# Attention block over 16 images on one core: v's transpositions in eight parts, biases in the evictions, x loaded ahead of v

## The chip, the cores and the metric

The kernel runs on one core of one Trainium2 chip. The metric is the device time of one execution in microseconds; lower is better. A core has five engines that work at the same time, each through its own queue and in order: TensorE (PE) multiplies matrices, VectorE (DVE) and ScalarE (ACT) work elementwise, GpSimd (POOL) and SyncE (SP) here mostly issue transfers.

## The reference

Group normalisation, attention over the 1,024 pixels of each image, projection, residual. Cut to what matters:

```python
# x: (16, 512, 32, 32) float32; 4 heads of 128 channels, 8 groups
xg = x.reshape(b, 8, -1)
h = (xg - mean(xg)) / sqrt(var(xg) + 1e-5)      # then * gamma + beta, per channel
qkv = qkv_w @ h + qkv_b                         # (1536, 512) weights, 1x1 convolution
q, k, v = split(qkv)                            # each 4 heads x 128 x 1024
p = softmax(q.T @ k * scale)                    # 1024 x 1024 per head
o = v @ p.T
out = x + proj_w @ o + proj_b
```

## The kernel before

**Score steps.** The main loop (around L2230) runs over images b, heads h and key blocks j: step s = 32 b + 8 h + j. A step has two halves, one for each half of the 1,024 queries. A half issues a score matmul (L1600), its exponential on ScalarE (L1606), the weighted sum with v of the step before (`po`, L1697), and then "halfway" units: matmuls of other products, which share TensorE with attention. VectorE adds the exponentials up to the softmax's divisor (`tot`, L1621). At the end of a head the divisor is turned (L1630, L1632 and on), spread by transfers, and divides `o` (L1710).

**The other products.** q, k, v of the next image and the projection of the last one are made by Strassen's scheme, seven products in place of eight, on two levels. Images 1 to 3 take q, k, v with two levels of it (`two_levels`). From image 4 on (`OLD = 4`) `thirds` makes q, k, v in two pairs of heads, eight groups per pair (`G` = 0 to 15), with x in three column ranges of 342, 342 and 340. A group is seven units in the order p1, p2, p6, p5, p7, p4, p3. ScalarE empties some of the accumulators (L1156, L1160, L1163; for the projection L634, L650, L802): with a copy, or with an activation that adds a bias where `BIASED` says so. VectorE adds others at L1221 (in `thirds`) or L804 (in `two_levels`). The last of a group is c22 = y + u3: p3 accumulates on the bank that c22 reads, so TensorE cannot start p3 before that addition has ended.

The groups' results `r` are added up by outer additions (`combine`; L1284, L1293). They form q and k directly; for v they form `vt` by L1306, one instruction for each row of channels, which also adds v's bias. `turn_v` turns `vt` by 32 x 32 blocks on VectorE (L1017), writes it to DRAM (`vd`, L1025) and reads it back into `v` (L1030), both on POOL's queue. All four transpositions of a pair are put into the list `pending` at the pair's group 6; the list is worked off unit by unit, and what is left of the second pair runs with the last unit of group 15.

**When.** The groups for image b + 1 begin at head 2 of image b and go on until head 1, key block 0, of image b + 1 itself; the first pair's group 7 falls in head 3, key block 4. The projection of image b - 1 (`proj_groups`, four groups) runs in head 1 of image b. `prepare` loads the residual from x in DRAM, 256 KB each; `finish` (L1569 to L1576) adds result, bias and residual (L1572), the second part (L1575), and stores (L1576). In the same head the next x is loaded on POOL's queue (`load_x`, L289), its sums are taken by ScalarE (L325 to L331), group statistics by VectorE (L353 to L365, one power on POOL at L359), and then x is normalised in place by ScalarE (L108) after the shift `sh` (L101). The order on each engine is that of the program text, but for the places where the text gives a priority or puts an instruction behind another.

**Pools that the change touches.** `xpool`: x as two tiles of two channel chunks; `ypool`: four single tiles of 128 x 512, shared by `vu`, residuals and early weights; `vt` in `opool`.

Of the kernel before, what the change touches and what calls it, by code (L numbers as in the profile page):

```python
# [208 lines left out]
BIASED = {0: (0, -1), 5: (2, 1), 14: (0, 1), 12: (2, 1)}  # L209
# [20 lines left out]
def fast_path(ctx, tc, x, sources, out, consts, flag, dims):  # L230
# [16 lines left out]
    xpool = ctx.enter_context(tc.tile_pool(name="x", bufs=KC))  # L247
# [8 lines left out]
    ypool = ctx.enter_context(tc.tile_pool(name="y", bufs=4))  # L256
# [22 lines left out]

    def load_x(b, chunks=range(NCC)):  # L280
        for c in chunks:
            if c % KC == 0:
                xw[b, c // KC] = xpool.tile([P, KC, N], F32, tag="x", name=f"x_{b}_{c // KC}")
            xs[b, c] = xw[b, c // KC][:, c % KC, :]
# [96 lines left out]

    def halves(tiles, prefix):

        b = {
            f"b{r + 1}{h + 1}": [tiles[2 * r + k][:, ts(h, HALF)] for k in range(KC)]
            for r in range(2) for h in range(2)
        }
        b["t1"] = b["b12"]
        for n in ("t2", "t3", "t4"):
            if prefix == "x":  # L390
                t = tpool.tile([P, KC, HALF], F32, tag="f", bufs=3, name=f"x{n}")
                b[n] = [t[:, k] for k in range(KC)]
                continue
            b[n] = [
                tpool.tile([P, HALF], F32, tag=f"{prefix}{n}{k}", name=f"{prefix}{n}{k}")
                if n == "t4" else home["A"][:, 2 * (int(n[1]) - 2) + k]
                for k in range(KC)
            ]
        return b
# [153 lines left out]
    def stage_v():  # L553
# [4 lines left out]
        for n in ("a21", "a22", "s4"):  # L558
            t = ypool.tile([P, HALF], F32, tag="y", name=f"wv_{n}")
            wv[n] = t.rearrange("p (k m) -> p k m", m=HC)  # L560
# [9 lines left out]
    def keep_kept(site, part, eng):  # L570
# [8 lines left out]
        if part == 0 and site == "proj":  # L579
            beside["s4"] = ypool.tile([P, HALF], F32, tag="y", name=f"k{site}_s4").rearrange(  # L580
                "p (f d) -> p f d", d=P
            )
# [105 lines left out]
    def two_levels(name, site, b, blocks, finish, sums="make", homes="BBBB", prepare=None):  # L688
# [59 lines left out]
        def group_units(g):  # L748
# [31 lines left out]
            def out_(which, a, c=None):  # L780
# [16 lines left out]
                with (  # L797
# [3 lines left out]
                    if c is None:  # L801
                        nc.scalar.copy(dst, view(a))  # L802
                    else:
                        latest["outer"] = nc.vector.tensor_add(dst, view(a), view(c))  # L804

            p1, p2, p6, p5, p7, p4, p3 = strassen(
                f"{name}_{g}", mm, out_, n * Q, seeded=not (b == 0 and site in range(PAIRS))
# [43 lines left out]
        def ready(g):  # L851
            for which in results.get(g, ()) if prepare else ():
                for r in range(2):
                    prepare(which, r)
# [11 lines left out]
        def done(which, i, j):  # L866
            pending.extend(
# [128 lines left out]
    def v_groups(b):  # L996
# [3 lines left out]
        def finish(which, h, a, c):  # L1000
            pair, half = int(which[1]) - 1, int(which[2]) - 1
            t = ypool.tile([P, HALF], F32, tag="y", name=f"vt_{b}_{pair}_{h}_{half}")
            i = 2 * pair + h
            nc.vector.scalar_tensor_tensor(t, a, vb_sb[:, i : i + 1], c, ALU.add, ALU.add)
            turn_v(b, pair, half, h, t, rows)
# [3 lines left out]
    def turn_v(b, pair, half, h, t, rows):  # L1009
        which = half  # L1010
        if (b, pair) not in vs:
            vs[b, pair] = vpool.tile(
                [P, NH2, 2, P, NB // NH2], F32, tag="v", name=f"v_{b}_{pair}"
            )
        n = P // BLK
        u = ypool.tile([P, HALF], F32, tag="y", name=f"vu_{b}_{pair}_{h}_{half}")
# [4 lines left out]
        if h == 0:  # L1021
            rows[which] = dpool.tile(
                [2 * P, HALF], F32, tag="v", name=f"vd_{b}_{pair}_{half}"
            )
        nc.gpsimd.dma_start(rows[which][ts(h, P), :], u)  # L1025
        if h == 0:
            return

        for q in range(n):
# [4 lines left out]
                rows[which].rearrange("(k m) (q e) -> q m k e", m=BLK, q=n)[q],  # L1034
            )

    def wide_x(b, r, n):
        return xw[b, r][:, :, ds(S3[n], W3)]

    def thirds(b):  # L1040

        first = b == old
        R, forms, made, sums, wts, rows, vts = {}, {}, {}, {}, {}, {}, {}
        pending, waiting = [], []
        late["heads"] = False
        count = len(THIRDS)
# [7 lines left out]
        def block(G, i, r, ch):  # L1054

            f = THIRDS[G % count][i]
            if f in RAW_B:
                row, n = RAW_B[f]
                return xw[b, row][:, r, ds(S3[n] + ch * H3, H3)]
            return forms[G][:, r, i, ts(ch, H3)]  # L1060

        def all_blocks(G, r, ch):
            return forms[G][:, r, : size(G), ts(ch, H3)]
# [25 lines left out]
        def make_sum(G, m):  # L1089
# [10 lines left out]
            def of(what, i=None):  # L1100
                if what[0] == "t":
                    return sums[G, what] if i is None else sums[G, what][:, i, :]
                r, ch = int(what[1]) - 1, int(what[2]) - 1
                return all_blocks(G, r, ch) if i is None else block(G, i, r, ch)

            with ExitStack() as order:
# [40 lines left out]
        def evict(dst, src, row, G):  # L1147
# [10 lines left out]
            for i, f in enumerate(group):  # L1158
                if f not in BIASED:
                    nc.scalar.copy(dst[:, i, :], src[:, i, :])  # L1160
                    continue
                m, sign = BIASED[f]
                nc.scalar.activation(  # L1163
                    dst[:, i, :], src[:, i, :], AF.Identity, bias=column(m, p, row, sign)
                )

        def column(m, p, row, sign=1):
            k = (HEADS if m else 0) + KC * p + row
            return negq[:, k : k + 1] if sign < 0 else qkb_sb[:, k : k + 1]
# [15 lines left out]
        def group_units(G):  # L1185
# [70 lines left out]
            def unit(k):  # L1256
                def one():
# [9 lines left out]
                    if G == 2 * count - 1 and k == len(us) - 1:  # L1267
                        run(f for _, f in pending)
# [3 lines left out]
            return [unit(k) for k in range(len(us))]  # L1272

        def combine(G):
# [13 lines left out]
            def final(m, n, add, i, j, frees=()):  # L1288
# [13 lines left out]
                def v(row):  # L1302
                    k = KC * p + row
                    if (p, row) not in vts:
                        vts[p, row] = opool.tile([P, N], F32, tag="o", name=f"vt_{b}_{p}_{row}")
                    nc.vector.scalar_tensor_tensor(  # L1306
                        vts[p, row][:, ds(S3[n], W3)], at(i, row), vb_sb[:, k : k + 1],
                        at(j, row), ALU.add, ALU.add if add else ALU.subtract,
                    )
                    if row:  # L1310
                        free(*frees)

                if m == 1:
                    pending.extend((G, lambda row=row: v(row)) for row in range(2))
                else:
                    pending.append((G, q_or_k))

            def alone(m, n, i, scale):

                def one():  # L1320
                    head_tiles(b, p)
                    for row in range(2):
                        dst = qw[b, p][m // 2][:, row, ds(S3[n], W3)]
                        nc.scalar.activation(
                            dst, at(i, row), AF.Identity, bias=column(m, p, row), scale=scale
# [10 lines left out]
            def turn(half, h):  # L1336
                def one():
                    turn_v(b, p, half, h, vts[p, h][:, ts(half, HALF)], rows_of_v)
                pending.append((G, one))
# [5 lines left out]
            elif g == 2:  # L1345
                op(False, 4, 2, 4, (2,))
                final(1, 0, True, 8, 3, (8,))
                op(True, 7, 7, 4)
                alone(2, 2, 7, -1.0)
# [3 lines left out]
            elif g == 4:  # L1353
                final(1, 2, False, 6, 4, (4,))
                op(False, 11, 11, 6, (6,))
            elif g == 5:
# [4 lines left out]
            elif g == 6:  # L1361
                final(1, 1, False, 10, 9, (10,))
                op(True, 9, 9, 13)
                rows_of_v = {}
# [13 lines left out]
    negq = one.tile([P, HEADS], F32, name="negq")  # L1378
# [118 lines left out]
    def lay_builder():  # L1497
# [7 lines left out]
        at(HEADS, 4, lambda: nc.scalar.mul(negq, qkb_sb[:, :HEADS], -1.0))  # L1505
# [37 lines left out]
    def proj_groups(b):  # L1543
# [3 lines left out]
        def place(which, r):  # L1547
            return 2 * (int(which[1]) - 1) + r, int(which[2]) - 1

        def prepare(which, r):  # L1550
            o, half = place(which, r)

            own = which == "c12"
            t = ys[which, r] = (tpool if own else ypool).tile(
                [P, HALF], F32, tag=f"ot4{r}" if own else "y", name=f"y_{b}_{o}_{half}"
            )

            eng = nc.sync if own else nc.gpsimd
            dma = eng.dma_start(t, x[b, ts(o, P), ts(half, HALF)])
# [9 lines left out]
        def finish(which, r, a, c):  # L1569
            o, half = place(which, r)  # L1570
            t = ys.pop((which, r))
            nc.vector.scalar_tensor_tensor(  # L1572
                t, a, projb_sb[:, o : o + 1], t, ALU.add, ALU.add
            )
            nc.vector.tensor_add(t, t, c)  # L1575
            latest["sent"] = nc.gpsimd.dma_start(out[b, ts(o, P), ts(half, HALF)], t)  # L1576
# [177 lines left out]
    def last_loads(what):  # L1754


        if what == "x":
            late["y"] = []
            for c in range(NCC):
                if c % KC == 0:  # L1760
                    two = xpool.tile([P, KC, N], F32, tag="x", name=f"y_{c // KC}")
                t = two[:, c % KC, :]
# [152 lines left out]
    def plan_head(b, h):  # L1915
# [23 lines left out]
        elif h == 1:  # L1939
            if b > 0:  # L1940
                spread(plan, [None] * 28, 0, NB)
                halfway.extend([flow.pop() if flow else []] + paced(proj_groups(b - 1), 3))
            if b + 1 == B:
                plan[0].append(lambda: last_loads("x"))
            else:
# [3 lines left out]
                spread(plan, [lambda c=c: stats_chunk(b + 1, c) for c in chunks], *at)  # L1949
# [280 lines left out]
    for s in range(steps + 1):  # L2230
# [15 lines left out]
        for half in range(NH2):  # L2246
# [23 lines left out]
            run(extras.pop((s, half), ()))  # L2270
        if s < steps and h == 1 and j == 6 and 0 < b < B - 1:
# [150 lines left out]
```

## Time and profile before

| | |
|---|---|
| median of 3 runs | 3164.6 us (3163.41 to 3168.26) |
| profiled execution: time, span | 3165.8 us, 3164.3 us |
| TensorE busy | 3122.8 us, 99% |
| VectorE busy | 2723.2 us, 86% |
| ScalarE busy | 1683.8 us, 53% |
| GpSimd busy | 520.8 us, 16% |
| data moved | 632.69 MB, 200 GB/s |
| granted TensorE clock | 9 tenths or more in all 40 slices |

Times are microseconds from the start of the span. In the timeline a row reads: start, time to the last end, engine, line, operation, output <- inputs, number of instructions run together, and in brackets the idle time before with what ended it. A matmul of this program is two records. Records of one engine overlap by a few hundredths to some tenths of a microsecond, so a duration is longer than the distance to the next start. In the waits a row reads: who waits, for whom, total, times, longest.

### The profile page before, as it was taken

The page shows a single profiled execution, that of the slowest core. Times are in us where ns is not written, and L with a number is a line of the kernel's source. Part 1 is how long each engine was busy: PE and PEld are TensorE (multiplying, and loading weights), DVE is VectorE, ACT ScalarE, POOL GpSimd, SP SyncE. Part 2 cuts the span into 40 slices and gives each one's busy share as a digit, 9 for nine tenths or more (in the row PEclk, how much of TensorE's full clock was granted, in tenths as well). Part 3 has the DMA queues.
Part 4 walks back from the last instruction along what each step waited for, and adds up shares of the span by engine and source line. Part 5 has one row for each costly group of instructions (what it writes and reads, how often), then busy time and mean ns, then how long its engine had stood idle before and what let it go on. Part 6 is the DMA issues. An engine that isn't in the chain of part 4 may idle for free. (4 is left out here: it accounts for less than half of the span.)

```text
span 3164.3 us, 38443 instructions
## 1 busy us (share of the span) xinstructions
PE 3122.8 (99%) x11934; PEld 2260.2 (71%) x11934; DVE 2723.2 (86%) x4792; ACT 1683.8 (53%) x3529; POOL 520.8 (16%) x935
## 2 busy tenths in 40 slices
PE   9999999999999999999999999999999999999999
PEld 7566676767677777677776777777777776777775
DVE  9988888789898897988979889798897988979797
ACT  3545446455464555655556555465554656546543
POOL 0121121111021110211112111121111112111110
PEclk9999999999999999999999999999999999999999
DMA  5565765656766666676666666666666665666651
GB/s 176 176 222 169 246 201 174 201 176 195 240 224 217 201 196 197 221 216 197 197 195 224 210 199 201 199 220 209 195 207 200 213 216 189 215 199 210 213 195 46
DMA packets 245713, 632.69 MB, mean 200 GB/s; under 512 B 35184, under 2 KB 80368, under 8 KB 245504
## 3 DMA queue, kind: packets, MB, share of 16 engines
q1 hardware_dynamic: 165152, 363.59, 37.7%
q0 software_dynamic: 67680, 232.26, 20.8%
q10 hardware_dynamic: 12672, 34.35, 3.3%
q8 instruction: 96, 1.57, 0.2%
q14 instruction: 113, 0.93, 0.1%
HBM read 458.36 MB, written 171.69 MB: 199 GB/s over the span
## 5 line engine op out<-in xcount | busy, mean ns | idle before, releaser
L1697 PE MATMUL po<-p,v 128*128 128x512 f32 x2048 | 1045.4, 592 | 0.0
L1600 PE MATMUL s<-qk,qk 128*128 128x512 f32 x2048 | 1045.1, 592 | 0.0
L1606 ACT ACTIVATE p<-s 128x512 f32<-128x512 f32 x1024 | 611.8, 597 | 533.3 <-PE s L1600 529.0
L1697 PEld LDWEIGHTS po<-p,v 128*128 128x128 f32 x2048 | 615.9, 301 | 374.8 <-issue 258.6
L1621 DVE TENSOR_TENSOR tot<-tot,p 128x1024 f32<-128x1024 f32 (+1 forms) x408 | 472.5, 1159 | 130.4 <-ACT p L1606 128.6
L1600 PEld LDWEIGHTS s<-qk,qk 128*128 128x128 f32 x2048 | 361.4, 189 | 54.6 <-issue 26.8
L1221 DVE TENSOR_TENSOR r<-t_y,t_u 128x342 f32<-128x342 f32 (+1 forms) x384 | 186.0, 484 | 122.9 <-PE t_y L1197 88.2
L1025 POOL DMA_DIRECT2D vd<-vu x120 | 65.7, 549 | 1122.6 <-DVE vu L1017 1113.2
L1284 DVE TENSOR_TENSOR r<-r,r 128x684 f32<-128x684 f32 x264 | 226.3, 865 | 2.0 <-DVE r L1221 0.5
L1197 PE MATMUL t_x<-home_A,w 128*128 128x171 f32 x1008 | 187.9, 308 | 1.8 <-DVE w L1471 1.8
L1197 PE MATMUL t_x<-home_B,w 128*128 128x171 f32 x1008 | 187.7, 308 | 0.0
L1197 PEld LDWEIGHTS t_x<-home_A,w 128*128 128x128 f32 x1008 | 161.5, 189 | 32.6 <-issue 19.9
L1197 PEld LDWEIGHTS t_x<-home_B,w 128*128 128x128 f32 x1008 | 161.6, 189 | 30.4 <-issue 19.9
L775 PE MATMUL pp_x<-home_B,w_proj 128*128 128x256 f32 x630 | 168.3, 384 | 12.0 <-ACT pp_u L634 12.0
L1156 ACT COPY t_u<-t_x 128x342 f32<-128x342 f32 (+1 forms) x240 | 100.1, 417 | 145.1 <-PE t_x L1197 134.1
L775 PEld LDWEIGHTS pp_x<-home_B,w_proj 128*128 128x128 f32 x630 | 117.2, 190 | 56.1 <-ACT pp_u L634 29.9
L1030 POOL DMA_DIRECT2D v<-vd x240 | 139.7, 589 | 82.2 <-DMA vd<-vu 39.5
L1576 POOL DMA_DIRECT2D out_y<-y x120 | 65.7, 548 | 461.5 <-DVE y L1575 453.9
L1197 PEld LDWEIGHTS t_z<-f,w 128*128 128x128 f32 x528 | 89.5, 190 | 51.9 <-issue 34.4
L1017 DVE STREAM_TRANSPOSE vu<-vt 128x512 f32<-128x512 f32 x120 | 123.3, 1104 | 1.2 <-DMA vd<-vu 1.1
L1197 PE MATMUL t_y<-f,w 128*128 128x171 f32 x528 | 102.8, 312 | 17.1 <-DVE r L1221 17.0
L108 ACT ACTIVATE x<-x,sh,sc 128x512 f32<-128x512 f32 x120 | 94.4, 815 | 35.4 <-DVE sh L101 33.7
(394 smaller groups left out, 5111.6 us busy)
## 6 DMA issues: line engine op xcount, KB each, us to landing
w<-kept SPq DMA_DIRECT2D x178, 512.0 KB, 3.9
w<-kept SPq DMA_DIRECT2D x178, 384.0 KB, 3.9
kept_t<-home_A POOLq DMA_DIRECT2D x96, 342.0 KB, 4.1
home_B<-kept_t SPq DMA_DIRECT2D x96, 342.0 KB, 3.0
rinv<-row ACTq DMA_DIRECT2D x63, 512.0 KB, 5.0
x<-in_x POOLq DMA_DIRECT2D x60, 512.0 KB, 6.2
vd<-vu POOLq DMA_DIRECT2D x120, 256.0 KB, 4.2
v<-vd POOLq DMA_DIRECT2D x240, 128.0 KB, 5.2
```

What stands on the lines that cost most here:

```text
L108: return self.nc.scalar.activation(xn, x, AF.Identity, bias=sh[:, i], scale=sc[:, i])
L775: latest["product"] = nc.tensor.matmul(acc[:, ts(i, Q)], have["w"][t][:, i, slot, :], inner(i, bn), start=(first and i == 0), stop=True, s ...
L1017: nc.vector.transpose(u.rearrange("p (q i j) -> p j q i", q=n, i=BLK), t.rearrange("p (j q i) -> p j q i", q=n, i=BLK),)
L1030: nc.gpsimd.dma_start(vs[b, pair][ts(q, BLK), half].rearrange("m h (k i) j -> m (h k) (i j)", k=n), rows[which].rearrange("(k m) (q e) -> ...
L1156: nc.scalar.copy(dst, src)
L1197: latest["product"] = nc.tensor.matmul(acc[:, ts(i, H3)], wts[G, t][:, i, slot, :], moving, start=(start and i == 0), stop=True, skip_grou ...
L1221: nc.vector.tensor_add(dst, view(a), view(c))
L1284: (nc.vector.tensor_add if add else nc.vector.tensor_sub)(at(o), a, c)
L1600: latest["score"] = nc.tensor.matmul(sc, ks[b, h][:, ts(j, P)], qs[b, h][:, ts(half, HALF)], start=True, stop=True)
L1606: exps[s] = nc.scalar.activation(ps[s][:, ts(half, HALF)], sc, AF.Exp, scale=SCALE)
L1621: added[b, h, j] = nc.vector.tensor_add(tot[b, h][:, i], tot[b, h][:, i], ps[s][:, i])
L1697: summed = nc.tensor.matmul(po[half], v_block(b, h, j), ps[s][:, i], start=(j == 0), stop=(j == NB - 1),)
```

## The change

- *Biases.* v's bias and the projection's bias are added when ScalarE empties the accumulators: `BIASED` gets more entries, with sums and differences of the q, k and v biases made once (`sum_biases`); `BIASED_PROJ` and `empty` do it for the projection. The accumulators of the groups concerned are emptied in two instructions, one per factor. The final addition for v becomes one plain addition of 128 x 684 for both rows; the projection's `finish` becomes two plain additions of 128 x 1024.
- *Transpositions of v.* Eight parts of 256 columns per pair: for both rows, part 0 after group 2, part 3 after group 4, parts 1 and 2 after group 6. `vt` and `vu` hold both rows; `vd` is written in transfers of 512 KB.
- *Residual and output* move in four transfers of 512 KB per image in place of eight of 256 KB, in two tiles of the pool and one own tile (`ot4`).
- *x* lies in one tile, `every_x`; differences of blocks that lie in x itself are one instruction of 128 x 342 instead of two of 128 x 171.
- *Order.* Loads of the next x are issued ahead of the second pair's reads of v; what is pending after group 15 runs two per half; the projection begins half a step earlier; the statistics' sums are put behind an exponential.

```diff
-BIASED = {0: (0, -1), 5: (2, 1), 14: (0, 1), 12: (2, 1)}
+BIASED = {0: "-q-v", 2: "v", 3: "v", 5: "k+v", 12: "k-v", 14: "q+v"}
+BIASED_PROJ = {2: 0, 3: 0, 7: 1}
...
-    ypool = ctx.enter_context(tc.tile_pool(name="y", bufs=4))
+    ypool = ctx.enter_context(tc.tile_pool(name="y", bufs=2))
...
+            def empty(dst, src, row):
...
+                if not prepare or not any(f in BIASED_PROJ for f in group):
+                    nc.scalar.copy(dst, src)
+                    return
+                for i, f in enumerate(group):
+                    if f not in BIASED_PROJ:
+                        nc.scalar.copy(dst[:, i, :], src[:, i, :])
+                        continue
+                    o = KC * BIASED_PROJ[f] + row
+                    nc.scalar.activation(
+                        dst[:, i, :], src[:, i, :], AF.Identity,
+                        bias=projb_sb[:, o : o + 1],
+                    )
...
-                if g in FORMS_B:
-                    nc.vector.tensor_sub(to, of(a), of(c))
-                else:
-                    for i in range(n):
-                        nc.vector.tensor_sub(to[:, i, :], of(a, i), of(c, i))
+                nc.vector.tensor_sub(to, of(a), of(c))
...
                     if G == 2 * count - 1 and k == len(us) - 1:
-                        run(f for _, f in pending)
+                        late["tail"] = [f for _, f in pending]
...
+        def turn_part(p, h, part):
+            half, q = divmod(part, 2)
...
+            nc.vector.transpose(
+                u[:, h].rearrange("p (q i j) -> p j q i", q=n, i=BLK)[:, ds(2 * q, 2)],
+                made["vt"][:, h, ts(part, Q)].rearrange("p (j q i) -> p j q i", q=n, i=BLK),
+            )
...
+            nc.gpsimd.dma_start(rows.rearrange("(h p) e -> p h e", h=KC), u)
...
+            if p == 0:
+                back()
+            else:
+                late["reads"].append(back)
...
-                    nc.vector.scalar_tensor_tensor(
-                        vts[p, row][:, ds(S3[n], W3)], at(i, row), vb_sb[:, k : k + 1],
-                        at(j, row), ALU.add, ALU.add if add else ALU.subtract,
+                    (nc.vector.tensor_add if add else nc.vector.tensor_sub)(
+                        made["vt"][:, :, ds(S3[n], W3)], at(i), at(j)
                     )
...
+                turn(0)
...
+                turn(3)
...
-                for half in range(NH2):
-                    for h in range(2):
-                        turn(half, h)
                 alone(0, 1, 9, 1.0)
+                turn(1, 2)
...
-            dma = eng.dma_start(t, x[b, ts(o, P), ts(half, HALF)])
+            dma = eng.dma_start(t, place(which)(x))
...
-            nc.vector.scalar_tensor_tensor(
-                t, a, projb_sb[:, o : o + 1], t, ALU.add, ALU.add
-            )
+            nc.vector.tensor_add(t, a, t)
             nc.vector.tensor_add(t, t, c)
...
-                halfway.extend([flow.pop() if flow else []] + paced(proj_groups(b - 1), 3))
+                halfway.extend(paced(proj_groups(b - 1), 3))
+                if flow:
+                    halfway[0] = flow.pop() + halfway[0]
...
-                spread(plan, [lambda c=c: stats_chunk(b + 1, c) for c in chunks], *at)
+                spread(plan, [
+                    lambda c=c: behind_exp(lambda: stats_chunk(b + 1, c)) for c in chunks
+                ], *at)
...
+            for _ in range(2):
+                if late.get("tail"):
+                    late["tail"].pop(0)()
+            if h == 1 and j > 0 and late.get("reads"):
+                run(late.pop("reads"))
```

More of the change, by code (lines that the diff above doesn't have):

```diff
@@ L394, in halves @@
             b[n] = [
[L395 to L398, printed above, removed]
+                home["A"][:, 2 * (int(n[1]) - 2) + k] for k in range(KC)
+            ] if n != "t4" else list(map(own_t4().__getitem__, ((slice(None), k) for k in range(KC))))
         return b
@@ L852, in ready @@
             for which in results.get(g, ()) if prepare else ():
-                for r in range(2):
-                    prepare(which, r)
+                prepare(which)
         pending = []
@@ L1021, in turn_v, with read_v @@
         if h == 0:
-            rows[which] = dpool.tile(
+            rows[half] = dpool.tile(
                 [2 * P, HALF], F32, tag="v", name=f"vd_{b}_{pair}_{half}"
             )
-        nc.gpsimd.dma_start(rows[which][ts(h, P), :], u)
-        if h == 0:
-            return
+        nc.gpsimd.dma_start(rows[half][ts(h, P), :], u)
+        if h == 1:
+            read_v(b, pair, half, rows[half])
+    def read_v(b, pair, half, rows):
+        n = P // BLK
+        if (b, pair) not in vs:
+            vs[b, pair] = vpool.tile(
+                [P, NH2, 2, P, NB // NH2], F32, tag="v", name=f"v_{b}_{pair}"
+            )
         for q in range(n):
@@ L1334, in alone, with turn @@
                 pending.append((G, now))
[L1336 to L1339, printed above, removed]
+            def turn(*parts_):
+                for h in range(2):
+                    for part in parts_:
+                        pending.append((G, lambda h=h, part=part: turn_part(p, h, part)))
             if g == 1:
@@ L1377, in fast_path, with sum_biases @@
     home_c = tpool.tile([P, 4 * H3], F32, tag="homeC", name="home_C")
-    negq = one.tile([P, HEADS], F32, name="negq")
+    biases = {"v": vb_sb}
+    for what in ("q+v", "-q-v", "k+v", "k-v"):
+        biases[what] = one.tile([P, HEADS], F32, name=f"bias_{len(biases)}")
+    def sum_biases():
+        q, k = qkb_sb[:, :HEADS], qkb_sb[:, HEADS:]
+        nc.vector.tensor_add(biases["q+v"], q, vb_sb)
+        nc.vector.tensor_scalar_mul(biases["-q-v"], biases["q+v"], -1.0)
+        nc.vector.tensor_add(biases["k+v"], k, vb_sb)
+        nc.vector.tensor_sub(biases["k-v"], k, vb_sb)
     for p_ in range(PAIRS):
```

147 lines of the change are left out of this document (86 added, 61 removed).

## The prediction

> **What bounds the kernel now.** I read the page's busy shares first, then the waits of TensorE, then the timeline of each place where TensorE waits.
>
> ```profile
> PE 3122.8 (99%) x11934; PEld 2260.2 (71%) x11934; DVE 2723.2 (86%) x4792; ACT 1683.8 (53%) x3529; POOL 520.8 (16%) x935
> ```
>
> ```profile
> PE t_y L1197 <- DVE r L1221: 17.9, 26, 1.9
> PE pp_x L775 <- ACT pp_u L634: 12.0, 24, 0.7
> ```
>
> TensorE bounds the whole span, and the change leaves its matmuls as they are. So the change can earn only what TensorE waits for, or spend by making new waits. Two waits carry nearly all: the last unit of a group of q/k/v (a `t_y` matmul), which needs the addition c22 that VectorE makes at L1221, and the last units of the projection, which need a copy by ScalarE. Both are queues being late, not engines being full: VectorE works in order, and what is put ahead of c22 delays it. The waits repeat in each image at three places, which I call A, B and C.
>
> **Place A** (head 3, key block 4, the last unit of the first pair's group 7). VectorE's timeline, then TensorE's:
>
> ```profile
> 1975.44 2.99 DVE L1017 STREAM_TRANSPOSE vu<-vt 128x512 f32<-128x512 f32 x3
> 1978.29 1.20 DVE L1621 TENSOR_TENSOR tot<-tot,p 128x1024 f32<-128x1024 f32 x1
> 1979.42 1.08 DVE L1017 STREAM_TRANSPOSE vu<-vt 128x512 f32<-128x512 f32 x1
> ...
> 1981.13 0.48 DVE L1221 TENSOR_TENSOR r<-t_y,t_u 128x342 f32<-128x342 f32 x1
> ```
>
> ```profile
> 1980.23 0.46 PE L1197 MATMUL t_x<-home_A,w 128*128 128x171 f32 x2
> 1980.52 0.74 PE L1197 MATMUL t_x<-x,w 128*128 128x171 f32 x4
> 1981.67 0.85 PE L1197 MATMUL t_y<-f,w 128*128 128x171 f32 x4 [0.40 <-DVE r L1221]
> 1982.35 1.02 PE L1600 MATMUL s<-qk,qk 128*128 128x512 f32 x2
> ```
>
> Instructions overlap, so I count from start to start. Two records take 0.29 us (1980.23 to 1980.52), four 0.58; `t_y` was due at 1981.10 and came at 1981.67. It then takes 0.68 instead of 0.58. The wait costs 0.57 + 0.10 = 0.67 us. It occurs once for each of the 12 images whose q/k/v go this way, the first time shorter: about 7.7 us. What is ahead of c22 is four transpositions, 2.85 / 3 = 0.95 each.
>
> **Place B** (head 1, key block 0, the last unit of the second pair's group 15):
>
> ```profile
> 2045.64 1.06 DVE L1306 SCALAR_TENSOR_TENSOR vt<-r,vb_sb,r 128x342 f32<-128x342 f32 x2
> 2046.73 0.87 DVE L1284 TENSOR_TENSOR r<-r,r 128x684 f32<-128x684 f32 x1
> 2047.52 3.93 DVE L1017 STREAM_TRANSPOSE vu<-vt 128x512 f32<-128x512 f32 x4
> 2051.27 1.23 DVE L1621 TENSOR_TENSOR tot<-tot,p 128x1024 f32<-128x1024 f32 x1
> ...
> 2053.41 0.50 DVE L1221 TENSOR_TENSOR r<-t_y,t_u 128x342 f32<-128x342 f32 x1
> ```
>
> ```profile
> 2052.78 0.31 PE L1197 MATMUL t_x<-home_B,w 128*128 128x171 f32 x1
> 2053.97 0.85 PE L1197 MATMUL t_y<-f,w 128*128 128x171 f32 x4 [0.89 <-DVE r L1221]
> 2054.66 1.02 PE L1600 MATMUL s<-qk,qk 128*128 128x512 f32 x2
> 2055.51 1.02 PE L1697 MATMUL po<-p,v 128*128 128x512 f32 x2
> ```
>
> Due at 2052.93 (one record, 0.145), come at 2053.97: 1.04 + 0.10 = 1.15 us, 12 times, 13.8 us.
>
> **Place C** (head 1, key blocks 5 to 7, the projection's last two groups). ScalarE, TensorE, VectorE:
>
> ```profile
> 1899.01 0.81 ACT L108 ACTIVATE x<-x,sh,sc 128x512 f32<-128x512 f32 x1 [2.64 <-DVE sh L101]
> 1899.73 0.35 ACT L634 COPY pp_u<-pp_x 128x256 f32<-128x256 f32 x1
> 1899.98 0.81 ACT L108 ACTIVATE x<-x,sh,sc 128x512 f32<-128x512 f32 x1
> ```
>
> ```profile
> 1896.43 0.59 PE L775 MATMUL pp_z<-o,w_proj 128*128 128x256 f32 x2
> 1896.86 0.59 PE L775 MATMUL pp_x<-home_B,w_proj 128*128 128x256 f32 x2
> ...
> 1899.01 0.59 PE L775 MATMUL pp_y<-home_B,w_proj 128*128 128x256 f32 x2
> 1900.13 0.70 PE L775 MATMUL pp_x<-home_B,w_proj 128*128 128x256 f32 x2 [0.53 <-ACT pp_u L634]
> ...
> 1902.99 0.70 PE L775 MATMUL pp_x<-home_B,w_proj 128*128 128x256 f32 x2 [0.45 <-ACT pp_u L634]
> ```
>
> ```profile
> 1891.68 0.19 DVE L354 STREAM_TRANSPOSE groups<-table 128x64 f32<-128x64 f32 x1
> 1891.79 0.38 DVE L740 TENSOR_TENSOR home_B<-o 128x256 f32<-128x256 f32 x1
> 1892.18 0.78 DVE L356 COPY groups<-groups 32x64 f32<-32x64 f32 x4
> ...
> 1893.61 1.01 DVE L357 BATCH_NORM_AGGREGATE groups<-groups 128x2 f32<-128x192 f32 x1
> ...
> 1901.35 1.29 DVE L1575 TENSOR_TENSOR y<-y,pp_r 128x512 f32<-128x512 f32 x2
> ```
>
> The copies stand behind normalisations of the next x (L108). A projection matmul takes 0.43 (1896.43 to 1896.86); the one due at 1899.44 came at 1900.13. With its slower start that is 0.79 us; the second wait costs about 0.71 and two small ones the rest, in all 1.88 us per image, in 11 images (the first of them 1.23): 20 us. A, B and C are 41.5 us.
>
> **The change, part by part.** Further rows:
>
> ```profile
> L1163 ACT ACTIVATE t_u<-t_x,qkb_sb 128x171 f32<-128x171 f32 x144 | 52.8, 403 | 52.1 <-PE t_x L1197 52.1
> L1324 ACT ACTIVATE qk<-r,qkb_sb 128x342 f32<-128x342 f32 x96 | 54.6, 582 | 10.4 <-DVE r L1284 10.4
> L325 ACT ACTIVATE junk<-x 128x1024 f32<-128x1024 f32 x60 | 63.3, 1055 | 3.6 <-DVE part L1632 2.6 <-DMA x<-in_x 0.7
> ```
>
> ```profile
> x<-in_x POOLq DMA_DIRECT2D x60, 512.0 KB, 6.2
> ...
> out_y<-y POOLq DMA_DIRECT2D x120, 256.0 KB, 3.0
> ...
> y<-in_x POOLq DMA_DIRECT2D x90, 256.0 KB, 4.9
> ```
>
> *Transpositions of v.* Four of 128x512 per pair become eight of 128x256; two run after group 2, two after group 4 and four after group 6. Only those four still stand ahead of c22 at A and at B. No row shows a 128x256 transposition of this layout. It lies between 0.11 us (128x64, 1891.68 to 1891.79) and 0.94 (128x512: 2047.52 to 2051.27 is 3.75 for four). A line through the two gives 0.47; I take 0.49, as the small one is the nearer row in form but not in stride. Four cost 1.96 instead of 3.75: 1.8 us less ahead of c22.
>
> [...]
>
> *Bias of v.* Two L1306 of 128x342 (2045.64 to 2046.73, 1.06 busy, spaced 0.49) become one addition of 128x684, 0.79 (2046.73 to 2047.52): 0.2 us less. The bias goes into ScalarE's evictions, which must be split for it. A biased 171-wide one lasts 0.40, a 342-wide one 0.58, a 256-wide one so about 0.49 (an estimate), 0.39 start to start, beside 0.25 for its plain half (1899.73 to the 1899.98 at which L108 goes on). ScalarE is at 53% and waits for TensorE before most evictions, so the 3 to 4 us that this adds per image are hidden except where a copy is awaited within its own time; I find no such place outside C and set 0, with 0.2 us per image as the upper bound.
>
> *A and B after.* c22 can start 1.8 + 0.2 = 2.0 us earlier as far as VectorE's queue goes. The stalls were 0.57 and 1.04. Both go, with the slow first matmul behind each: 7.7 + 13.8 = 21.5 us. Next late is the copy that c22 itself reads, which at other groups leaves over half a microsecond. The two transpositions after group 4 come before c22 of group 5; there 0.98 new less what vt saves leaves an estimated 0.2 us in hand. After group 12 the queue has idle time before its next sum, so nothing follows:
>
> ```profile
> 1837.25 1.22 DVE L1621 TENSOR_TENSOR tot<-tot,p 128x1024 f32<-128x1024 f32 x1 [2.46 <-ACT p L1606]
> ```
>
>
> *Projection: bias in the eviction, 128x1024 residual additions, half a step earlier; statistics behind the exponential.* Eight plus eight additions of 128x512 become four plus four of 128x1024, bias and residual in one chain. In the new order the normalisations of x no longer stand before the last copies, so C's waits on ScalarE go. But VectorE's order is new: from the exponential of key block 4's second half on there stand ahead of c22 of the projection's last group the sum tot, the division of o, the halves' addition and four residual additions (7 x 1.13, the spacing 1978.29 to 1979.42), a memset and small transposition 0.14, c12 0.60 (1.29 - 0.69 of the L1575 pair), four copies 0.8, the aggregate 0.93, small ones 0.37; with c22's own 0.42, 11.2 us. TensorE, from the end of that score, has 9 passes of 0.85 (2054.66 to 2055.51) and 10 matmuls of 0.43 until it needs c22: 12.0 us. The exponential ends between 0.6 us after its score, if ScalarE is free, and 1.7, behind a copy's two parts (0.64) and a statistics pass (1.05, L325). The order puts both ahead, so I take 1.7: c22 is 0.9 us late, with the slow start 1.0 to 1.1. Bounds 0 and 1.6. C goes from 1.88 to 1.1 in 11 images: 20 - 12 = 8 us saved.
>
> *Loads.* x ahead of the second pair's v: ScalarE waited 0.7 us in all for x, so earlier x earns nothing. The v reads come some 2 us later on POOL's queue, but v of the second pair is used from head 2 on, over 30 us later. Fewer, larger stores and loads: nothing, hidden by the same distance, except in the second rival. *Last outer additions two per half, merged differences, one x tile:* VectorE's work off the critical path; 0.
>
> **Sum.** 7.7 + 13.8 + 8 = 29.5 us. The profiled execution took 3165.8 us (span 3164.3); the median of the runs is 1.2 below. 3165.8 - 29.5 = 3136.3: I say 3136.
>
> **Rivals.**
> *1. A half-size transposition costs what a full one does*, 0.94. Then only vt's 0.2 is saved: A waits 0.42 + 0.10, B 0.85 + 0.10, group 5 gets a new wait of about 0.75, C stays at 1.1: 3.3 us per image instead of 3.7, 3160. For it: both would be bound by a fixed part. Against: 128x64 takes 0.11. Chance 0.10. Each 0.1 us on the price beyond 0.72 (B's limit) brings back some 0.4 us per place.
>
> *2. Slower: the residual for c21 lands too late.* The double tile of c11 is stored and loaded again for c21; VectorE's addition to c21 stands ahead of c22 of the last group and of the shift by which x is normalised. VectorE has about 12 us of work between the two, so nothing waits if store and load of 512 KB take under that: 3.0 + 4.9 us, the rows for 256 KB, up to 6.2 + 6.2, that of 512 KB, with 1.1 for the issues. At 16 us, by crowded queues, each of 11 images loses 3.8 more: 3136 + 42 = 3178. It is slower than before from about 15 us on. For it: POOL's queue holds the load until the store has landed, and stores behind it. Against: 6.2 for 512 KB is well under the 7.5 that each of the two would need. Chance 0.10; with other late queues of that kind 0.14.
>
> *3. C is gone altogether*, the exponential being early: 3136 - 12 = 3124. Chance 0.20.
>
> **How the numbers follow.** The forecast, with C between 0.5 and 1.6 us (3130 to 3142), has 0.50; 3124 has 0.20; rival 1 0.10, half of it within 0.2% (6.3 us, about what a measurement tells from no change); several small waits that eat half of the gain, 3145 to 3158, 0.06; slower 0.14. The range 3120 to 3160 leaves out the slower cases and little more. Faster 0.50 + 0.20 + 0.05 + 0.06 = 0.81, same 0.05, slower 0.14.
>
> **What would show it.** The waits of TensorE for c22 of q/k/v should fall from 17.9 us to about 3, those for the projection's copies from 12 to 1 or 2, and a new wait of the projection's `pp_y` for VectorE should stand at about 9 us in 11 places. The transposition's group should show 240 of 128x256 at 0.55 to 0.65 us. Wrong is the forecast if these are 0.9 or more, if `t_y` still waits a dozen times, or if VectorE idles for a DMA ahead of the residual additions.

## The result and the profile after

The changed kernel takes 3151.3 us (median of 5 runs, 3149.2 to 3154.5), the kernel before 3164.6 (5 runs): ratio 0.9958, interval 0.9943 to 0.9972. It is faster, by 13 us where 28.6 were forecast. Its profiled execution has a span of 3151.3 us against 3164.3.

Busy shares and the waits of TensorE (who waits for whom, total, times, longest) in the changed kernel:

```profile
PE 3112.6 (99%) x11934; PEld 2265.1 (72%) x11934; DVE 2699.6 (86%) x4604; ACT 1724.2 (55%) x3744; POOL 476.2 (15%) x782
```

```profile
PE pp_y L779 <- DVE pp_r L808: 21.3, 16, 1.5
PE t_y L1232 <- DVE r L1256: 7.2, 5, 4.1
```

The wait for c22 of q, k, v fell from 17.9 us in 26 places to 7.2 in 5. The waits for ScalarE's copies of the projection (12.0 us) are gone. In their place stands a wait that the kernel before did not have: the projection's last unit for VectorE, 21.3 us.

**Place A**, VectorE's timeline, then TensorE's:

```profile
1972.58 2.07 DVE L1317 STREAM_TRANSPOSE vu<-vt 128x256 f32<-128x256 f32 x4
1974.49 1.21 DVE L1685 TENSOR_TENSOR tot<-tot,p 128x1024 f32<-128x1024 f32 x1
1975.70 0.51 DVE L1256 TENSOR_TENSOR r<-t_y,t_u 128x342 f32<-128x342 f32 x1
```

```profile
1977.07 0.74 PE L1232 MATMUL t_x<-x,w 128*128 128x171 f32 x4
1977.65 0.74 PE L1232 MATMUL t_y<-f,w 128*128 128x171 f32 x4
```

Four transpositions take 1.91 us up to the next start, and c22 ends at 1976.21. `t_y` starts 0.58 after `t_x`, which is the pace of four records: no wait. **Place B** likewise:

```profile
2043.40 2.06 DVE L1317 STREAM_TRANSPOSE vu<-vt 128x256 f32<-128x256 f32 x4
...
2047.93 0.51 DVE L1256 TENSOR_TENSOR r<-t_y,t_u 128x342 f32<-128x342 f32 x1
```

```profile
2048.21 0.75 PE L1232 MATMUL t_x<-home_B,w 128*128 128x171 f32 x4
2048.80 0.74 PE L1232 MATMUL t_y<-f,w 128*128 128x171 f32 x4
```

**Place C**: VectorE from the sum tot of key block 4 to c22 of the projection's last group, ScalarE's two results that they wait for, and TensorE:

```profile
1888.17 1.22 DVE L1685 TENSOR_TENSOR tot<-tot,p 128x1024 f32<-128x1024 f32 x1
1889.31 1.22 DVE L1774 TENSOR_TENSOR o<-o,rinv 128x1024 f32<-128x1024 f32 x1
...
1892.12 1.22 DVE L882 TENSOR_TENSOR pp_r<-pp_r,pp_r 128x1024 f32<-128x1024 f32 x1
1893.27 1.01 DVE L360 BATCH_NORM_AGGREGATE groups<-groups 128x2 f32<-128x192 f32 x1
1894.20 1.16 DVE L1638 TENSOR_TENSOR y_c<-pp_r,y_c 128x1024 f32<-128x1024 f32 x1
...
1895.34 1.21 DVE L1638 TENSOR_TENSOR y_c<-pp_r,y_c 128x1024 f32<-128x1024 f32 x1
1897.01 0.24 DVE L366 STREAM_TRANSPOSE groups<-groups 128x64 f32<-128x64 f32 x1 [0.46 <-POOL groups L362]
1897.17 1.18 DVE L1639 TENSOR_TENSOR y_c<-y_c,pp_r 128x1024 f32<-128x1024 f32 x1
...
1898.35 1.22 DVE L1639 TENSOR_TENSOR y_c<-y_c,pp_r 128x1024 f32<-128x1024 f32 x1
...
1899.56 0.42 DVE L808 TENSOR_TENSOR pp_r<-pp_y,pp_u 128x256 f32<-128x256 f32 x1
```

```profile
1887.53 0.59 ACT L1670 ACTIVATE p<-s 128x512 f32<-128x512 f32 x1
...
1894.72 0.47 ACT L823 ACTIVATE pp_u<-pp_x,projb_sb 128x256 f32<-128x256 f32 x1 [1.13 <-PE pp_x L779]
```

```profile
1885.48 1.02 PE L1664 MATMUL s<-qk,qk 128*128 128x512 f32 x2
...
1897.52 1.02 PE L1761 MATMUL po<-p,v 128*128 128x512 f32 x2
1900.03 0.70 PE L779 MATMUL pp_y<-o,w_proj 128*128 128x256 f32 x2 [1.48 <-DVE pp_r L808]
```

ScalarE's copy is ready at 1895.19, over four microseconds before VectorE comes to use it. VectorE is busy without a break but for 0.46 us, in which it waits for the power that GpSimd computes. `pp_y` was due at 1898.38 (0.86 after `po`) and came at 1900.03: 1.65 us late. This happens in all 14 images that have such a projection beside the next x.

**Image 4**, whose weights are built while its groups run (one time per execution), VectorE and TensorE:

```profile
808.27 0.86 DVE L1347 TENSOR_TENSOR r<-r,r 128x684 f32<-128x684 f32 x1
814.73 0.42 DVE L1536 TENSOR_TENSOR w<-w 128x256 f32<-128x256 f32 x1 [5.59 <-DMA w<-kepta]
...
816.19 0.50 DVE L1256 TENSOR_TENSOR r<-t_y,t_u 128x342 f32<-128x342 f32 x1
```

```profile
811.88 0.74 PE L1232 MATMUL t_x<-f,w 128*128 128x171 f32 x4
816.74 1.51 PE L1232 MATMUL t_y<-x,w 128*128 128x171 f32 x4 [4.12 <-DVE r L1256]
818.05 1.91 PE L1664 MATMUL s<-qk,qk 128*128 128x512 f32 x2
819.75 1.91 PE L1761 MATMUL po<-p,v 128*128 128x512 f32 x2
```

A weights' sum waits 5.59 us on VectorE for its load, and c22 of group 8 is queued behind it, though it needs nothing of that load. In the kernel before, c22 stood ahead of such a sum:

```profile
809.60 0.54 DVE L1221 TENSOR_TENSOR r<-t_y,t_u 128x342 f32<-128x342 f32 x1
813.31 0.43 DVE L1469 TENSOR_TENSOR w<-w 128x256 f32<-128x256 f32 x1 [3.16 <-DMA w<-in_qkv_wT]
```

When TensorE goes on in the changed kernel, its records take twice as long: the score, 1.70 start to start instead of 0.86.

Counted as the prediction did, as start-to-start time over the pace of back-to-back records (0.145, 0.216 and 0.429 us), TensorE lost 59.9 us before and 47.3 after, the opening 9 us left out. The 12.6 us less are made of 19.7 won at A and B from image 5 on, 2.3 lost in new short waits at group 5 of the same images, 1.8 lost at the projection (0.7 in images 4 to 14, 0.9 in images 1 to 3, 0.2 in the last), 3.9 lost in image 4, and small ones of both signs, 0.9 won in all.

### The profile page after: what moved, and what is told of

It is laid out like the page before. It is cut to its first block, busy times and chain, and to the rows that moved or that the text cites. A ratio compares the mean times of both kernels' runs of the same rounds, so it can differ in the third digit from the quotient of the medians.

```text
span 3151.3 us, 38222 instructions
## 1 busy us (share of the span) xinstructions
PE 3112.6 (99%) x11934; PEld 2265.1 (72%) x11934; DVE 2699.6 (86%) x4604; ACT 1724.2 (55%) x3744; POOL 476.2 (15%) x782
## 4 chain that ended last, share of the span: by engine, by line
PE 51%; DVE 3%; DMA 1%; issue 1%; POOL 0%; ACT 0%; POOLq 0%; DVEq 0%
PE po L1761 15%; PE s L1664 15%; PE t_x L1232 9%; PE t_y L1232 5%; PE pp_x L779 2%; PE t_z L1232 2%; PE pp_y L779 1%; DMA x<-in_x 1%; PE pp_z L779 1%; DVE y_c L1639 1%; DMA y_c<-in_x 0%; DVE tot L1685 0%; POOL groups L362 0%; DVE o L1774 0%; DVE pp_r L808 0%
## 5 line engine op out<-in xcount | busy, mean ns | idle before, releaser
L1325 POOL DMA_DIRECT2D vd<-vu x48 | 34.8, 727 | 967.2 <-DVE vu L1317 967.2
L1119 DVE TENSOR_TENSOR f<-x 128x684 f32<-128x684 f32 x168 | 143.3, 853 | 0.8
L1192 ACT COPY t_u<-t_x 128x342 f32<-128x342 f32 x192 | 78.7, 410 | 117.7 <-PE t_x L1232 112.6
L1317 DVE STREAM_TRANSPOSE vu<-vt 128x256 f32<-128x256 f32 x192 | 104.2, 644 | 0.0
L1157 POOL DMA_DIRECT2D kept_t<-home_A x96 | 52.5, 547 | 333.6 <-DVE home_A L1150 326.4
```

The costliest lines, as they stand in the source:

```text
L1119: (eng.tensor_add if op == "+" else eng.tensor_sub)(made[f], of(a), of(c))
L1192: nc.scalar.copy(dst, src)
L1317: nc.vector.transpose(u[:, h].rearrange("p (q i j) -> p j q i", q=n, i=BLK)[:, ds(2 * q, 2)], made["vt"][:, h, ts(part, Q)].rearrange("p ( ...
```

## The experiments

They ran on other chips, where the kernel before took 3168.4 to 3168.9 us; so each is given by its ratio to the kernel before on its own chip. The changed kernel's ratio, measured where the kernel before took 3164.6 us, is 0.9958.

**Was it the transpositions at A and B?** All else kept, four whole ones per pair after group 6:

```diff
-                turn(0)
...
-                turn(3)
...
-                turn(1, 2)
+                for half in range(NH2):
+                    for h in range(2):
+                        pending.append((G, lambda h=h, half=half: turn_part(p, h, half)))
...
-                u[:, h].rearrange("p (q i j) -> p j q i", q=n, i=BLK)[:, ds(2 * q, 2)],
-                made["vt"][:, h, ts(part, Q)].rearrange("p (j q i) -> p j q i", q=n, i=BLK),
+                u[:, h].rearrange("p (q i j) -> p j q i", q=n, i=BLK),
+                made["vt"][:, h, ts(half, HALF)].rearrange("p (j q i) -> p j q i", q=n, i=BLK),
```

> The changed kernel with four transpositions of 128x512 per pair after group 6, as in the kernel before, and all else of the change kept. By the built order four of them stand ahead of c22 at A and at B, and v's addition is the merged one (0.2 us shorter). Theory: the half-size transpositions are what freed A and B; waits of 0.4 us at A and 0.85 at B, plus 0.1 each, come back in 11 or 12 images: 17 us slower than the changed kernel, 3168. Rival: the biases' additions that left VectorE freed them; then within 3 us of 3151.

Measured: 0.9999 (0.9990 to 1.0009), 3167.0 us. The whole gain is gone. TensorE at A and at B:

```profile
1980.92 0.85 PE L1232 MATMUL t_y<-f,w 128*128 128x171 f32 x4 [0.23 <-DVE r L1256]
```

```profile
2053.24 0.85 PE L1232 MATMUL t_y<-f,w 128*128 128x171 f32 x4 [0.90 <-DVE r L1256]
```

Against the pace A loses 0.40 and B 1.06, with 0.10 each for the slow first matmul. So the half-size pieces freed A and B, and the moved biases alone did not. The pieces also cost something: with whole ones the short waits at group 5 (2.3 us) are gone, and image 4's stretch loses 7.0 us, near the 7.5 before, instead of 11.4. So the pieces won 18.5 us at A and B and lost 6.7 elsewhere.

**Is it their place in the text?** All eight parts put after group 6:

```diff
-                turn(0)
...
-                turn(3)
...
-                turn(1, 2)
+                turn(0, 1, 2, 3)
```

> The changed kernel with all eight transpositions of a pair after group 6 instead of 2, 2 and 4. Theory: places A and B were late by the transpositions ahead of c22; eight of about 0.5 us are 4 us, as much as the four of 128x512 before, so the waits of 0.5 us at A and 1.0 at B (plus 0.1 each) come back in 12 images: about 20 us slower, 3171. Rival: A and B went because v's bias left VectorE and the rest of the queue got shorter; then at most 5 us slower, 3151 to 3156.

Measured: 0.9953 (0.9937 to 0.9970): no change; the expectation fell. VectorE's timeline shows why:

```profile
1937.11 0.66 DVE L1317 STREAM_TRANSPOSE vu<-vt 128x256 f32<-128x256 f32 x1
1941.81 0.64 DVE L1317 STREAM_TRANSPOSE vu<-vt 128x256 f32<-128x256 f32 x1
1955.86 0.65 DVE L1317 STREAM_TRANSPOSE vu<-vt 128x256 f32<-128x256 f32 x1
1958.30 0.57 DVE L1317 STREAM_TRANSPOSE vu<-vt 128x256 f32<-128x256 f32 x1
1971.00 2.08 DVE L1317 STREAM_TRANSPOSE vu<-vt 128x256 f32<-128x256 f32 x4
```

Two parts follow the first column range of `vt` (made at 1934.76) and two the third (1953.80), though the text names all eight after group 6; four remain ahead of c22, as in the changed kernel. So the parts whose columns are ready early run early, wherever the text names them. The cut into parts makes that possible; the three places in the text do not matter. I had taken the text's place for the engine's: that the order on each engine is the text's, as the description of the kernel has it, does not hold here.

**Place C: what makes c22 late?** Three runs. First the residual additions of c21 and c12 behind the last outer additions:

```diff
-                pending.append(lambda: finish(which, part(*i), part(*j)))
+                step = lambda: finish(which, part(*i), part(*j))
+                (pending if which in ("c11", "c22") else held).append(step)
...
+                    with tc.issue_after(latest["outer"].ins) if held else nullcontext():
+                        run(held)
```

> The changed kernel (3151.3 us) waits 1.65 us (plus 0.10) in each of 14 images for c22 of the projection's last group. Theory Q: c22 is late because VectorE's queue ahead of it is long (11.4 us from the sum tot of key block 4). Here the residual additions of c21 and c12 are put behind the last group's outer additions; by the built order two 128x1024 additions leave the queue ahead of c22 (2.27 us), one tot (1.13) and one 128x512 addition (0.60) move in: c22 0.5 us earlier, the wait about 1.1 us, 3144. Rival D: the addition to c21 waits for its residual's load; then the whole wait goes, 3127. Rival S: ScalarE's copy is what is late; then nothing changes, 3151.

Measured: 0.9961 (0.9947 to 0.9975), no gain. TensorE's waits:

```profile
PE pp_y L779 <- DVE pp_r L808: 14.1, 16, 1.0
PE t_y L1236 <- DVE r L1260: 12.3, 16, 3.7
```

The wait at C did fall as theory Q says, 1.65 to 1.11 us, which excludes a late residual load and a late ScalarE. But c22 of q, k, v, which had 7.2 us in 5 places, now waits 12.3 in 16: the work that was put off made group 5 of the next pair late. The time was moved, not won.

Then the statistics, not put behind the exponential:

```diff
-                    lambda c=c: behind_exp(lambda: stats_chunk(b + 1, c)) for c in chunks
+                    lambda c=c: stats_chunk(b + 1, c) for c in chunks
```

> The changed kernel with the statistics' sums not put behind the exponential. In the built order the four copies, the aggregate and the shift then stand ahead of the sum tot of key block 4, so about 2 us (0.8 + 0.9 + the wait for GpSimd's power 0.46) leave the stretch between that sum and c22 of the projection's last group. Theory Q: the wait of 1.65 us falls to 0 or nearly, 14 x 1.6 = 22 us, 3129, if the normalisations do not stand ahead of the projection's copies again; if they do, the waits of the kernel before at that place (1.9 us) come back, 3153. Rival S (ScalarE late, by the exponential): 3140 to 3150, with the wait in the same place.

Measured: 0.9904 (0.9887 to 0.9920), 3138.1 us. TensorE's wait and VectorE's timeline:

```profile
PE pp_y L779 <- DVE pp_r L808: 5.8, 14, 0.4
```

```profile
1878.21 1.01 DVE L360 BATCH_NORM_AGGREGATE groups<-groups 128x2 f32<-128x192 f32 x1
...
1881.01 1.22 DVE L1685 TENSOR_TENSOR tot<-tot,p 128x1024 f32<-128x1024 f32 x1
...
1890.96 0.42 DVE L808 TENSOR_TENSOR pp_r<-pp_y,pp_u 128x256 f32<-128x256 f32 x1
```

The aggregate now stands ahead of tot, and from tot to c22 it is 9.95 us instead of 11.39. Theory Q had expected some 2 us less and no wait; it is 1.44 less, and against the pace a wait of 0.58 us stays. Waits of 0.1 for ScalarE's copies, with their slow starts, take a little of the gain. Of the 13 us, 10.6 are won at the projection and 2.2 at group 5, whose short waits go too. The queue is the cause, and putting the statistics behind the exponential is the part of the change that lengthened it.

Last the projection's start at its old half step:

```diff
-                halfway.extend(paced(proj_groups(b - 1), 3))
-                if flow:
-                    halfway[0] = flow.pop() + halfway[0]
+                halfway.extend([flow.pop() if flow else []] + paced(proj_groups(b - 1), 3))
```

> The changed kernel with the projection begun half a step later, as in the kernel before. By the built order the shift of x then comes ahead of the four residual additions, and ten 128x1024 passes and more stand ahead of c22 of the projection's last group, while TensorE needs it half a step (2.6 us) later. Theory Q (the queue decides): the wait of 1.65 us stays between 1 and 2 us, or ScalarE's copies are late again behind the normalisations as in the kernel before (1.9 us): 3147 to 3155. Rival: the half step is what the change lost at this place; the wait goes, 3128 to 3135.

Measured: 0.9962 (0.9947 to 0.9976), 3154.4 us, as theory Q has it: the waits of the projection move back to ScalarE's copies and to several places of 0.1 to 0.6 us, 1.75 us per image, as much as in the changed kernel.

**Image 4: what makes c22 late?** Two runs. The reads of v later, in case they crowd out the load:

```diff
+            if p == 0 and first:
+                extras.setdefault((NB * HEADS * b - 3, 0), []).append(back)
```

> The changed kernel with the reads of v of the first pair of image 4 issued some 10 us later (three steps before image 4 begins). In the changed kernel TensorE waits 4.1 us at 812 to 817 us for a load of weights that takes 9 to 11 us beside these reads, and then runs 5 us at half clock. Theory: the reads, bunched by the transpositions' new order, crowd out that load; the wait falls by 2 to 4 us and the slow stretch (2 us) goes: 3145 to 3147. Rival: the load is late for the other transfers (weights, differences of x), then 3151.

Measured: 0.9950 (0.9934 to 0.9967), 3152.2 us, not to be told from the changed kernel; the expected 5 us did not come. The wait is shorter by 0.67 us only, so crowding is not the main cause; but the half clock is gone (granted clock 1.00 at 816 to 820 us, 0.50 in the changed kernel):

```profile
816.73 0.85 PE L1232 MATMUL t_y<-x,w 128*128 128x171 f32 x4 [3.45 <-DVE r L1256]
```

The weights' sums behind the c22 of the group before:

```diff
-                inner_weights(w, size(G))
+                with tc.issue_after(made["c22"].ins):
+                    inner_weights(w, size(G))
```

> The changed kernel with the sums of image 4's weights put behind the addition c22 of the group before. In the changed kernel such a sum waits on VectorE 5.6 us for its load, and c22 is queued behind it; in the kernel before c22 stood ahead of it. Theory: that order is the cause of the 4.1 us wait at 812 to 817 us; the wait falls to about 2 us, as in the kernel before, TensorE keeps its clock (2 us), and the wait of 1.35 us at 803 us goes: 5 us less, 3146. Rival: the load itself is late, TensorE then waits as long for the weights: 3150 to 3151.

Measured: 0.9927 (0.9910 to 0.9943), 3145.8 us. VectorE and TensorE:

```profile
811.16 0.51 DVE L1257 TENSOR_TENSOR r<-t_y,t_u 128x342 f32<-128x342 f32 x1
814.13 0.43 DVE L1539 TENSOR_TENSOR w<-w 128x256 f32<-128x256 f32 x1 [2.46 <-DMA w<-kepta]
```

```profile
816.42 0.85 PE L1233 MATMUL t_x<-home_A,w 128*128 128x171 f32 x4 [0.38 <-DVE w L1541]
```

The load lands no sooner (814.1 against 814.7), but c22 no longer stands behind its wait, and TensorE waits 0.38 us. What is lost in this stretch falls from 11.4 to 2.6 us. 2.5 us more appear in image 1, where TensorE's clock fell after a wait of 2.2 us (see the last section). The order was the cause.

**Loads of x ahead of v, undone:**

```diff
-            if p == 0:
-                back()
-            else:
-                late["reads"].append(back)
+            back()
```

> The changed kernel with the second pair's reads of v issued as soon as v is written, ahead of the loads of x as in the kernel before. The prediction gave this part nothing, as ScalarE hardly waits for x: 3150 to 3153, the wait for c22 of the projection's last group the same 1.65 us. Rival: the loads of x ahead matter; then ScalarE's statistics come late and the time rises by more than 6 us.

Measured: 0.9941 (0.9925 to 0.9958), 3150.6 us; the wait at C stays 1.65. This part of the change is worth nothing, as forecast.

**A version that beats both.** The statistics not behind the exponential, and the weights behind c22:

> The changed kernel with the statistics not behind the exponential, and the sums of image 4's weights behind c22. The statistics alone brought about 13 us (3138), the weights' sums are expected to bring 5 more where theory holds: 3133. If the weights' order is not the cause, 3138.

Measured: 0.9893 (0.9877 to 0.9910), 3133.4 us. With c21's and c12's additions behind as well:

> The version with the statistics not behind the exponential and image 4's weights behind c22 (3133 us), with c21's and c12's residual additions behind the last group's outer additions as well. By the built order two 128x1024 additions leave the queue ahead of c22 (2.27 us), a tot (1.13) and a 128x684 difference (0.78) move in: c22 0.36 us earlier. Theory Q: the wait left there, 0.58 us, falls to about 0.2, 14 x 0.36 = 5 us: 3128, if nothing else becomes late; if the additions put off delay a group later, as alone they did, 3131 to 3135.

Measured: 0.9887 (0.9871 to 0.9904), 3132.8 us. At C the wait falls from 0.58 to 0.35, but the gain in time is within the intervals.

## Why the prediction was wrong

**Right: A and B.** Forecast 21.5 us less, some 1.5 of them in image 4; measured 19.7 from image 5 on. Image 4's share is lost in its stretch. The price of the step with no row of its own held: 0.49 us forecast, an estimate between the rows of 128x64 and 128x512; 1.91 / 4 = 0.48 measured. The group:

```profile
L1317 DVE STREAM_TRANSPOSE vu<-vt 128x256 f32<-128x256 f32 x192 | 104.2, 644 | 0.0
```

(192 of them, not 240: 24 pairs by eight.) Rival 1, a half-size piece at the price of a whole one, is thereby excluded: 0.48 us for 256 columns is 1.9 ns a column, and the 0.94 for 512 columns in the kernel before is 1.8. (A transposition of 128x1024 into a contiguous tile, L1694, took 1.16 us start to start, 1.1 ns a column.) The forecast's reason was too narrow, though: that the parts have places of their own in the text proved idle.

**Wrong: the term of C, "C goes from 1.88 to 1.1 in 11 images".** This is the larger failure. The mechanism was named rightly, VectorE's queue ahead of c22, and the run with c21 and c12 put off shows it. Its size was not. The queue's sum was 11.2 us; it is 11.8 from tot's start to c22's end. Missing were the 0.46 us that VectorE waits for GpSimd's power, for which the sum has no term, as if the chain from the aggregate through GpSimd and back were hidden; and some 0.2 of small differences. The exponential ended 1.78 after its score, not 1.7. So the wait is 1.65 + 0.10 instead of 1.0 to 1.1, beyond the bound of 1.6. And the count was short: the same queue is late in the projections beside images 1 to 3 too, 14 in all, which I had left as before. In place of 8 us won, 1.8 were lost: this is about 10 of the 15 to 17 us that are missing.

**Wrong: image 4 as unchanged.** I gave the stretch where image 4's weights are built no term, since the change does not touch its lines. But the order on VectorE changes there too: in the built order a weights' sum that waits for a load came to stand ahead of c22. That is 3.9 us lost where the first A and B were to win about 1.5. It is the wait that takes the place of others, one place away from where I looked for it.

**Small:** the two parts after group 4 were to leave 0.2 us in hand at group 5; they do not quite, 0.1 us with its slow start is lost there, 2.3 us from image 5 on.

**Rivals.** 2, c21's residual landing late, did not occur: VectorE's idle time for such loads is 3.4 us in the whole trace, and it had none at C. 3, C gone altogether, was not the case, but with the statistics ordered otherwise the kernel comes near that time: 0.9904 of 3164.6 is 3134. The statement that loads of x ahead earn nothing held.

## What to carry to other kernels

Where one engine is at 99% and the others work in order, count each queue from the last thing that all wait for to the instruction that the busy engine needs, with each hop to another engine in it; here the 0.46 us wait for GpSimd's power counted in that chain as much as the work. Cutting the long transposition into parts gave the order room, and that was worth 0.4% here (0.9958 against 0.9999); the statistics' sums put behind an exponential of ScalarE lengthened VectorE's queue (11.39 us against 9.95). And after a change look at every place where an instruction that waits for a load shares a queue with one that doesn't (5.59 us here), also at those that no edit touches.

## What the runs showed of the hardware

TensorE's granted clock fell to half after some waits of these runs, and the length of the wait alone did not decide it. A window of the changed kernel, and the same place with the reads of v later (columns: busy time and count of PE, PEld, DVE, ACT and POOL, granted clock, DMA share, GB/s):

```profile
816.00:820.00 4.00, 3.26 (x7) 2.23 (x8) 3.70 (x7) 0.00 (x1) 0.00 (x0) 0.50 0.72 235
```

```profile
816.00:820.00 4.00, 3.27 (x14) 2.55 (x15) 3.69 (x7) 0.63 (x2) 0.00 (x0) 1.00 0.78 252
```

After 3.45 us idle the clock stayed at 1.00 here; after 3.75 (the run with c21 and c12 behind), 3.81 (all parts after group 6), 3.83 (the statistics) and 4.12 (the changed kernel) it fell, to 0.67, 0.50, 0.53 and 0.50 on the mean of the same window. In the changed kernel this cost 2.6 us: from `t_y` to the second score behind it are 6.16 us (816.74 to 822.90), and 3.57 with the reads of v later. But in image 1 much shorter waits were enough: 2.2 us in the run with the weights behind c22, and 1.87 in the one with the projection's old half step, which is shown first. After 1.97 us at the same place in the run with statistics and weights, shown second, the clock stayed up: its mean over the whole run is 1.000.

```profile
246.38 1.13 PE L779 MATMUL qk_y<-x,w 128*128 128x256 f32 x4 [1.87 <-DVE qk_r L808]
248.00:250.00 2.00, 2.00 (x4) 0.84 (x3) 1.93 (x5) 0.60 (x1) 2.00 (x4) 0.50 0.83 274
```

```profile
246.34 1.13 PE L779 MATMUL qk_y<-x,w 128*128 128x256 f32 x4 [1.97 <-DVE qk_r L808]
```

In the changed kernel's trace the clock changes at whole multiples of 3.4133 us from its first rise at 6.23: it falls at 815.19, rises at 822.02 and falls at 3149.91, 237, 239 and 921 of them later. Counted by such stretches, each fall came at the end of one in which TensorE was idle for long, 2.57 us of the wait of 4.12 and 2.30 us behind its last matmul; none of those before the two, nor any between them, has more than 1.55 us. In the kernel before the most up to the last matmul is 1.82 us, and the clock did not fall. Near that amount the runs differ: 1.87 us was enough in the run with the old half step, 1.97 in the one with statistics and weights was not; what decides there stays open. The wait of 3.45 us (813.28 to 816.73) is longer than a stretch, so it lay across two at least; if these begin as in the changed kernel, one of them at 815.19, it is an estimated 1.91 and 1.54 us in each. Then where in its stretch a wait falls would matter as well as its length.
